# A macaron block on one core: results split by expert order, more transfer slots late in attention, row scatters issued together

## The chip, the cores and the metric

The kernel runs on one core of a Trainium2 chip. The core has a matrix engine (TensorE, here PE), a vector engine (VectorE, DVE), an activation engine (ScalarE, ACT), a general engine (GpSimd, POOL) and a queue engine (SyncE, SP), each with its own instruction stream, and 16 DMA engines that move data between the on-chip memory and HBM. Engines wait for each other through semaphores. The metric is the device time of one launch in microseconds, the median of several executions.

## The reference

The input x is eight sequences of 512 tokens with 128 features. Three steps are added to it, one after the other:

```python
x = x + 0.5 * ffn(layernorm(x), router_w, router_b, W1, b1, W2, b2)
x = x + attention(layernorm(x), w_qkv, w_o, log_xi)
x = x + 0.5 * ffn(layernorm(x), router_w, router_b, W1, b1, W2, b2)
```

`ffn` is a mixture of eight experts, each `relu(x @ W1 + b1) @ W2 + b2` with 512 hidden features. A token goes to the two experts with the highest logits, and their results are added with the softmax of the two logits as gates. `attention` is causal with 16 heads of 8 features, half of them with rotary positions, half of them with a linear decay by distance.

## The kernel before

**Rows by expert.** Each ffn runs over groups of two or three sequences: f0, f1, f2 ahead of attention and g0 (sequences 0, 1), g1 (2, 3, 4), g2 (5, 6, 7) after it. For each sequence `route` (from L801) makes the layernorm, the logits, the two chosen experts and, per token and choice, a row `g.to` in a table `xs` in HBM. Row numbers hold the expert in their lowest three bits: row = place x 8 + expert. Eight scatters a sequence (L875, an indirect DMA from POOL, 128 rows each) bring the normalised rows there. `experts` (from L924) then fetches each expert's rows (`fetch`, L933), transposes them, multiplies by W1 and W2 in "pieces" (PE lines 976, 989, 1013), and adds the bias on the way out of PSUM (L1017, on DVE, into `ysb`).

**Two ways back.** The results of f0 to f2 and g0 are written in expert order and gathered per token by indirect DMAs (`combine`). The groups g1 and g2 are "tagged": each row of `xs` carries two more values, a row number of its token (`xn[:, :, D]`, the row of the first choice) and a place for the result (`xn[:, :, D + 1]`, from `place`). `homes` (L943 to L951) finds from them, on DVE, where in `ys` the result of each row belongs: token after token, and for each token first choice, then second. `send` (L957) scatters 120 result rows at a time there, from POOL. `collect` (from L1099) reads the two results of each token back with plain DMAs from SP (L1110) and adds them to x with the gates (L1114, one instruction a choice and 128 tokens), then stores x (L1120). For g1 it does so within the run of units, for g2 at the very end, in two parts a sequence:

```python
while m.results:
    m.transfer()
last = [m.collect(g2, i, out, parts=2) for i in range(3)]
step(*last)
run(*last)
```

**Order by hand.** PE, ACT, DVE and SP execute in program order. The program is a run of units: -30 to -1 ahead of attention, 0 to 95 attention (a sequence has 12), up to 125 after it; `core` is 96, `tail` 108 and `ends` 126. `surround(n, att)` makes one unit: attention's matmuls, then a quota of pieces of the ffn group whose turn it is, mixed with what is due (routing, projections, collecting). g1 fills units 79 to 106 and g2 units 107 to 125.

**Transfers.** Indirect DMAs are not issued where they arise. Row scatters and gathers enter the queue `jobs`, result scatters the queue `results`, and `transfer()` issues one: from `jobs` first, or, with `second=True`, from `results` unless a job is urgent or there are more than four jobs and no result. A unit has two such slots, one after its first piece and one at its end; from unit `core` on a third lies in the middle if over two transfers are waiting. Each indirect DMA also waits for `mark`, the last evacuation of PSUM (or mask operation) ahead of it in the program. On POOL, scatters keep their place relative to all other instructions but not to each other. POOL also computes `rstd` of each layernorm.

**The last sequence.** Sequence 7 leaves attention in unit 98. Its routing follows in units 99 to 102, three steps a unit: statistics, `rstd`, normalisation; transposes, logits, ranks; places and gates; its eight scatters enter the queue in unit 101. g2's first rows are fetched at the end of unit 105, and the fetch waits for all scatters.

Of the kernel before, what the change touches and what calls it, by code (L numbers as in the profile page):

```python
# [11 lines left out]
FP = mybir.dt.float32  # L12
BF = mybir.dt.bfloat16
I32 = mybir.dt.int32
# [434 lines left out]
class Group:  # L449


    def __init__(self, seqs, cap, key, xs, ys, tagged):
        self.seqs, self.cap, self.key, self.xs, self.ys = seqs, cap, key, xs, ys
        self.tagged, self.width = tagged, D + 2 * tagged
        self.ct = -(-cap // P)
        self.rows = cap // self.ct
        assert self.ct * self.rows == cap
        self.parts = [(t, min(3 if cap > 4 * P else 4, self.ct - t))
                      for t in range(0, self.ct, 3 if cap > 4 * P else 4)]
        self.placed = 0  # L460
        self.pieces = E * (len(self.parts) * (1 + C) + self.ct) + 1


# [19 lines left out]
class Main:  # L483
    def __init__(self, tc, ctx, aps):
# [52 lines left out]
        for e in range(4):  # L537
# [4 lines left out]
            if e == 2:  # L542
# [48 lines left out]
                       allow_small_or_imprecise_dtypes=True)  # L591

        self.place = const.tile([P, T], FP, name="place")
        nc.gpsimd.iota(self.place, [[2 * P, T]], base=0, channel_multiplier=2,
                       allow_small_or_imprecise_dtypes=True)

        self.row = {}
# [203 lines left out]
    def route(self, g, i, urgent=False, ahead=False, early=False):  # L801
# [60 lines left out]
        for r in range(2):  # L862
            nc.vector.scalar_tensor_tensor(
                sm[:, :, r, :], rank, float(r), posb, ALU.is_equal, ALU.mult
            )
        nc.vector.tensor_reduce(g.to[:, i], sm, AX.X, ALU.max)
        nc.vector.tensor_scalar(g.back[:, i], g.to[:, i], E * g.cap - 1, None, ALU.min)
        if g.tagged:
            nc.vector.tensor_copy(xn[:, :, D], g.to[:, i, :, 0])
            nc.vector.tensor_scalar(  # L870
                xn[:, :, D + 1], self.place, float(2 * N * i), None, ALU.add
            )

        def scatter(t, r):
            ins = nc.gpsimd.indirect_dma_start(  # L875
# [35 lines left out]
        nc.vector.tensor_scalar(tot, e2, 1.0, 2.0, ALU.add, ALU.mult)  # L911
        nc.vector.reciprocal(g.gates[:, i, :, 0], tot)
        nc.vector.tensor_tensor(g.gates[:, i, :, 1], g.gates[:, i, :, 0], e2, ALU.mult)
        yield

    def close_group(self, g, k):
# [7 lines left out]
    def experts(self, g):  # L924
# [14 lines left out]
        def homes(e, xb):  # L939

            row = self.row[g.cap][:rows]
            second = self.small.tile([P, CT], FP, tag="second", name=f"second_{key}_{e}")
            nc.vector.scalar_tensor_tensor(  # L943
                second[:rows, : g.ct], xb[:rows, : g.ct, D], -float(e), row,
                ALU.add, ALU.not_equal,
            )
            nc.vector.tensor_tensor(
                second[:rows, : g.ct], second[:rows, : g.ct], xb[:rows, : g.ct, D + 1], ALU.add
            )
            home[e] = self.small.tile([P, CT], I32, tag="home", bufs=7, name=f"home_{key}_{e}")  # L950
            nc.vector.scalar_tensor_tensor(  # L951
                home[e][:rows, : g.ct], row, float(2 * N * len(g.seqs) + e),
                second[:rows, : g.ct], ALU.add, ALU.min,
            )

        def send(e, t, ys):
            ins = nc.gpsimd.indirect_dma_start(  # L957
                out=g.ys[:, :],
                out_offset=bass.IndirectOffsetOnAxis(ap=home[e][:rows, t : t + 1], axis=0),
                in_=ys[:rows, t, :], in_offset=None,  # L960
            ).ins
            tc.declare_no_dep(ins, group=f"ys_{key}", reason="no two rows have the same home")
            tc.add_to_no_dep_group(f"ys_{key}", ins)
            self.in_turn(ins, scatter=True)
            self.behind_mark(ins)

# [72 lines left out]
        for e in range(E):  # L1039
            if e + 1 < E:  # L1040
                h_next, turns, wides_next = up(e + 1, loaded.pop(0))
            else:
                turns = []

            rest = downs[:1] + turns + downs[1:]
            last = turns[-1] if turns else None
            for i, piece in enumerate(wides):
                piece()
                yield
                k = -(-len(rest) // (len(wides) - i)) if rest else 0  # L1050
                for other in rest[:k]:
                    other()
                    if other is last and e + 3 < E:
                        loaded.append(fetch(e + 3))
                    yield
                rest = rest[k:]
            downs = down(e, h)
            if e + 1 < E:
                h, wides = h_next, wides_next
        for piece in downs:  # L1060
            piece()
            yield
# [36 lines left out]
    def collect(self, g, i, dst, parts=1):  # L1099

        nc = self.nc
        b = g.seqs[i]
        x = self.x[b]
        if i % 2 == 0:
            self.pair = self.p2.tile([P, 2, T, 2, D], FP, tag="ee", name=f"yr_{b}")
        yr = self.pair[:, i % 2]
        src = g.ys[2 * N * i : 2 * N * (i + 1), :].rearrange("(t p r) d -> p t r d", p=P, r=2)
        n = T // parts
        for k in range(parts):
            nc.sync.dma_start(yr[:, ts(k, n)], src[:, ts(k, n)])  # L1110
        yield
        for t in range(T):
            for r in range(2):
                nc.vector.scalar_tensor_tensor(  # L1114
                    x[:, t, :], yr[:, t, r], g.gates[:, i, t, r : r + 1], x[:, t, :],
                    ALU.mult, ALU.add,
                )
            if t % n == n - 1:
                k = t // n
                nc.sync.dma_start(  # L1120
                    dst[b].rearrange("(t p) d -> p t d", p=P)[:, ts(k, n)], x[:, ts(k, n)]
                )
            if parts == 1:
                yield
# [179 lines left out]
def macaron_kernel(  # L1304
# [24 lines left out]
    def run(*streams):  # L1329
        for s in streams:  # L1330
            for _ in s:
                pass
# [23 lines left out]
    with ExitStack() as main:  # L1356
# [8 lines left out]
        g0 = m.open_group([0, 1], 351, 1, "g0")  # L1365
        g1 = m.open_group([2, 3, 4], 480, 3, "g1")
        g2 = m.open_group([5, 6, 7], 480, 4, "g2")
        order = [f0, f1, f2, g0, g1, g2]
        place = {True: {}, False: {}}
        for g in order:  # L1370
# [56 lines left out]
        def surround(n, att):  # L1427

            m.unit = n
            now = None  # L1430
            for g, fetch, start, end in plan:
                if n == fetch:
                    close(g)
                    fills[g.key] = [opened(g), g.pieces]
                if n == end:
                    run(fills[g.key][0])
                if start <= n < end:
                    now, until = fills[g.key], end
                    if g is g1 and att:
                        until = end + 7  # L1440
            quota = min(now[1], -(-now[1] // (until - n))) if now else 0
            fill = now[0] if now else iter(())
            if now:
                now[1] -= quota
            if att:
                ee = m.scores(*units[n])
            last, m.oT = m.oT, None
            if m.held is not None:
                got = m.values(*m.held)
                if got is not None:  # L1450
                    m.oT = (*m.held[:2], got)
            m.held = (*units[n], ee) if att else None
            m.evac = "dve" if att and n % seq not in (8, 9, 10) else "act"
            run(take(fill, 1 if quota else 0))
            m.evac = "act"
            if att:
                m.causal(units[n][2], ee, 0)
            m.transfer()
            if last is not None:
                m.outputs(*last)  # L1460
            if att:
                m.causal(units[n][2], ee, 1)
            if not att:
                m.additions()
            work = due.pop(n, [])
            todo = max(quota - 1, 0)
            for k, (stream, steps) in enumerate(work):
                some = todo // (len(work) - k + 1)
                run(take(stream, steps))
                run(take(fill, some))  # L1470
                todo -= some
            if n >= core and len(m.jobs) + len(m.results) > 2:
                run(take(fill, todo // 2))
                todo -= todo // 2
                m.transfer(second=True)
            run(take(fill, todo))
            m.additions()
            m.transfer(second=True)
# [54 lines left out]
        with m.banks(("m", 8)):  # L1533
            for u in range(core + 2, ends):
                surround(u, False)
            run(fills["g2"][0])
            assert not due, due
            assert not m.jobs and not m.adds
            while m.results:
                m.transfer()  # L1540
            last = [m.collect(g2, i, out, parts=2) for i in range(3)]
            step(*last)
            run(*last)

    flag = nc.values_load(
        bad[0:1, 0:1], min_val=0, max_val=1,
# [50 lines left out]
```

## Time and profile before

| | |
|---|---|
| median of three runs | 715.75 us (713.97 to 718.7) |
| profiled execution | 700.09 us, span 698.3 us |
| PE busy | 629.2 us (90%) |
| DVE busy | 410.2 us (59%) |
| ACT busy | 341.3 us (49%) |
| POOL busy | 300.3 us (43%) |
| result scatters, L957 | 64, 996 ns each on POOL |
| row scatters of g0 to g2, L875 | 64, 998 ns each on POOL |

The span runs from the first to the last instruction of one profiled execution. The page has the busy time of each engine and a picture of the span in 40 slices, each digit a busy share in tenths; PEclk is the clock that PE was granted, in tenths of full speed. Other answers of the trace are busy times in chosen stretches, instructions in order of time (start, duration, engine, line, operation, output and inputs, then in brackets the idle time of the engine before it and what ended it) and the chain of work that ended last, followed back from the end.

### The profile page before, as it was taken

The numbers are of one execution on the slowest core, as the hardware profiler recorded it, in microseconds if no ns is written. First come the engines' busy times: TensorE is split into PE (matmuls) and PEld (weight loads), VectorE is DVE, ScalarE is ACT, GpSimd is POOL, SyncE is SP. The second block draws the span as 40 slices with busy tenths as digits, with TensorE's granted clock in tenths as the row PEclk, the third lists the DMA queues.
The fourth block names the chain that finished last, engine by engine and source line by source line (L and its number), as shares of the span: only waits on it lengthen the run. The fifth ranks groups of instructions, "written<-read, shape, count | busy, mean of one in ns | idle before, by whom it ended". The sixth has DMA issues, their size and how long they took to land. (4 is left out here: it accounts for less than half of the span.)

```text
span 698.3 us, 13045 instructions
## 1 busy us (share of the span) xinstructions
PE 629.2 (90%) x4867; PEld 410.3 (59%) x4867; DVE 410.2 (59%) x1442; ACT 341.3 (49%) x548; POOL 300.3 (43%) x322
## 2 busy tenths in 40 slices
PE   3269999999999999999999999999999998969980
PEld 2148867756465656556656656656456656747760
DVE  6736448734466666675687677676666654433414
ACT  4034443455755656565665565555665552234420
POOL 3744637642223223314154423424144556575660
PEclk9999999999999999999999999999999999889995
DMA  8747843312409921111211111101402111145324
GB/s 265 197 136 209 205 115 98 85 45 77 101 22 172 264 69 38 30 29 43 71 32 49 40 38 38 30 27 39 105 27 75 35 31 42 53 121 140 104 58 143
DMA packets 78670, 61.06 MB, mean 87 GB/s; under 512 B 7392, under 2 KB 70792, under 8 KB 78600
## 3 DMA queue, kind: packets, MB, share of 16 engines
q1 hardware_dynamic: 69608, 42.51, 23.8%
q0 software_dynamic: 8704, 17.63, 8.5%
q8 instruction: 41, 0.67, 0.4%
q14 instruction: 29, 0.24, 0.1%
q10 hardware_dynamic: 288, 0.01, 0.0%
HBM read 26.34 MB, written 33.78 MB: 86 GB/s over the span
## 5 line engine op out<-in xcount | busy, mean ns | idle before, releaser
L1208 ACT ACTIVATE ee<-st 128x768 f32<-128x768 f32 (+1 forms) x192 | 159.0, 881 | 104.1 <-PE st L1201 100.6
L474 POOL DMA_INDIRECT yt_f<-ys,back_f x64 | 64.8, 1013 | 133.5 <-DVE ee L1215 55.7
L1215 DVE TENSOR_TENSOR ee<-ee,keep 128x256 f32<-128x256 f32 (+1 forms) x192 | 93.5, 507 | 25.4 <-ACT ee L1208 25.3
L1013 PEld LDWEIGHTS y_g<-w_sb,h_g 128*120 128x120 f32 (+1 forms) x704 | 87.1, 184 | 27.4 <-issue 21.7
L875 POOL DMA_INDIRECT xs<-xn_g,to_g x64 | 63.8, 998 | 90.1 <-DVE ee L1215 34.9
L1013 PEld LDWEIGHTS y_f<-w_sb,h_f 128*120 128x120 f32 (+1 forms) x704 | 85.9, 182 | 28.5 <-issue 16.2
L1201 PE MATMUL st<-qT,kT 32*128 32x512 f32 (+3 forms) x1024 | 96.1, 467 | 2.3 <-ACT h_f L996 0.8
L1013 PE MATMUL y_f<-w_sb,h_f 128*120 128x128 f32 (+1 forms) x704 | 93.9, 277 | 0.2 <-DVE h_f L998 0.2
L989 PE MATMUL z_g<-xT_g,w_sb 128*128 128x480 f32 (+1 forms) x192 | 92.6, 569 | 1.3 <-ACT xT_g L980 1.3
L1013 PE MATMUL y_g<-w_sb,h_g 128*120 128x128 f32 (+1 forms) x704 | 93.0, 277 | 0.6 <-DVE o_tok L1250 0.3
L1227 PE MATMUL o<-ee,vpad 128*32 128x512 f32 (+3 forms) x1024 | 89.4, 442 | 0.8 <-DVE ee L1215 0.8
L989 PE MATMUL z_f<-xT_f,w_sb 128*128 128x480 f32 (+1 forms) x192 | 88.8, 551 | 1.0 <-ACT xT_f L980 1.0
L996 ACT ACTIVATE h_f<-z_f,b1T 128x480 f32<-128x480 f32 (+1 forms) x86 | 53.5, 623 | 68.2 <-PE z_f L989 67.3
L957 POOL DMA_INDIRECT ys<-ysb_g,home_g x64 | 63.7, 996 | 39.3 <-ACT h_g L996 8.7
L1017 DVE TENSOR_TENSOR ysb_f<-y_f,b_sb 120x128 f32<-120x128 f32 (+1 forms) x88 | 25.0, 287 | 77.9 <-PE y_f L1013 74.2
L996 ACT ACTIVATE h_g<-z_g,b1T 128x480 f32<-128x480 f32 (+1 forms) x71 | 45.7, 646 | 47.4 <-PE z_g L989 46.7
L1201 PEld LDWEIGHTS st<-qT,kT 32*128 32x128 f32 x1024 | 43.1, 183 | 32.6 <-issue 8.1
L1017 DVE TENSOR_TENSOR ysb_g<-y_g,b_sb 120x128 f32<-120x128 f32 (+1 forms) x88 | 25.1, 287 | 58.2 <-PE y_g L1013 57.6
L1227 PEld LDWEIGHTS o<-ee,vpad 128*32 128x32 f32 x1024 | 23.5, 108 | 52.4 <-issue 7.5
L875 POOL DMA_INDIRECT xs<-xn_n,to_f x40 | 39.0, 974 | 34.9 <-ACT xi_sb L727 8.1
L989 PEld LDWEIGHTS z_g<-xT_g,w_sb 128*128 128x128 f32 x192 | 30.1, 195 | 26.6 <-issue 15.2
L989 PEld LDWEIGHTS z_f<-xT_f,w_sb 128*128 128x128 f32 x192 | 30.2, 194 | 13.8 <-issue 7.2
(186 smaller groups left out, 778.7 us busy)
## 6 DMA issues: line engine op xcount, KB each, us to landing
w_sb<-in_L_ffn_W_dram SPq DMA_DIRECT2D x16, 256.0 KB
xs<-zeros SPq DMA_DIRECT2D x8, 487.5 KB
xb_g<-xs SPq DMA_DIRECT2D x16, 243.8 KB
xb_f<-xs SPq DMA_DIRECT2D x16, 240.0 KB
ys<-ysb_f SPq DMA_DIRECT2D x16, 240.0 KB
ys<-zeros SPq DMA_DIRECT2D x2, 1536.0 KB
x<-in_L_attn_x_dram SPq DMA_DIRECT2D x8, 256.0 KB
xs<-zeros SPq DMA_DIRECT2D x1, 1920.0 KB
```

What stands on the lines that cost most here:

```text
L474: ins = op(*args, **kw)
L875: ins = nc.gpsimd.indirect_dma_start(out=g.xs[:, :], out_offset=bass.IndirectOffsetOnAxis(ap=g.to[:, i, t, r : r + 1], axis=0), in_=xn[:, ...
L957: ins = nc.gpsimd.indirect_dma_start(out=g.ys[:, :], out_offset=bass.IndirectOffsetOnAxis(ap=home[e][:rows, t : t + 1], axis=0), in_=ys[:r ...
L989: nc.tensor.matmul(z[:, :n], self.w1_sb[:, e, ts(c, P)], xT[:, n0 : n0 + n], start=True, stop=True,)
L996: ins = nc.scalar.activation(dst, z[:, :n], AF.Relu, bias=bias)
L1013: nc.tensor.matmul(y[:rows], h[:, c, ts(t, rows)], self.w2_sb[:, e, c, :], start=(c == 0), stop=(c == C - 1),)
L1017: ins = nc.vector.tensor_tensor(ys[:rows, t, :], y[:rows], self.b2_sb[:rows, e], ALU.add)
L1201: nc.tensor.matmul(st[:, h, c0 : c0 + N - kt * P], kT[r0 : r0 + SLOT, ts(kt, P)], qT[r0 : r0 + SLOT, kt * P :], start=True, stop=True,)
L1208: nc.scalar.activation(ee[:, two, :width], st[:, two, :width], AF.Exp)
L1215: ins = self.nc.vector.tensor_tensor(d, d, self.keep.unsqueeze(1).unsqueeze(1).to_broadcast([P, 2, len(parts), P]), ALU.min,)
L1227: self.nc.tensor.matmul(self.o[h * SLOT : (h + 1) * SLOT, kt * P :], self.vpads[b % 2][:, kt, 4 * g + h, :], ee[:, h, c0 : c0 + n], start= ...
```

## The change

It has three parts.

Results in two halves: the tag of a row becomes the row number of the token's lower-numbered expert, and the place is the token's number alone. `homes` adds the number of tokens of the group for a row of the higher expert, so that all lower results of a group lie in one half of `ys` and all higher ones in the other. The gates are swapped to match. `collect` reads the halves with one DMA each. For g2 (`g.ends`) it has more steps: the read of the lower half is issued before the last expert's W2 products, after the result queue has been emptied; expert 7 is no token's lower one, and its scatters are declared free of dependence on those reads. The higher half is read after the last scatter, then follow the additions of the lower half and those of the higher with the stores.

A third slot: the middle slot exists from unit 79 on, not from `core`.

Rows together: from unit `core + 2` on, the middle slot issues two more transfers if more than one job is waiting.

```diff
-        nc.gpsimd.iota(self.place, [[2 * P, T]], base=0, channel_multiplier=2,
+        nc.gpsimd.iota(self.place, [[P, T]], base=0, channel_multiplier=1,
...
         nc.vector.tensor_reduce(g.to[:, i], sm, AX.X, ALU.max)
+        if g.tagged:
+            which = small.tile([P, T, 2], I32, tag="which", name=f"which_{key}")
+            nc.vector.tensor_scalar(which, g.to[:, i], E - 1, None, ALU.bitwise_and)
+            swap = small.tile([P, T], FP, tag="swap", name=f"swap_{key}")
+            nc.vector.tensor_tensor(swap, which[:, :, 0], which[:, :, 1], ALU.is_gt)
+            apart = small.tile([P, T], FP, tag="apart", name=f"apart_{key}")
+            nc.vector.tensor_tensor(apart, g.to[:, i, :, 1], g.to[:, i, :, 0], ALU.subtract)
+            nc.vector.tensor_tensor(apart, apart, swap, ALU.mult)
+            nc.vector.tensor_tensor(xn[:, :, D], apart, g.to[:, i, :, 0], ALU.add)
+            nc.vector.tensor_scalar(xn[:, :, D + 1], self.place, float(N * i), None, ALU.add)
         nc.vector.tensor_scalar(g.back[:, i], g.to[:, i], E * g.cap - 1, None, ALU.min)
-        if g.tagged:
-            nc.vector.tensor_copy(xn[:, :, D], g.to[:, i, :, 0])
-            nc.vector.tensor_scalar(
-                xn[:, :, D + 1], self.place, float(2 * N * i), None, ALU.add
-            )
...
+        if g.tagged:
+            lo, hi = g.gates[:, i, :, 0], g.gates[:, i, :, 1]
+            nc.vector.tensor_tensor(tot, hi, lo, ALU.subtract)
+            nc.vector.tensor_tensor(tot, tot, swap, ALU.mult)
+            nc.vector.tensor_tensor(lo, lo, tot, ALU.add)
+            nc.vector.tensor_tensor(hi, hi, tot, ALU.subtract)
...
-            nc.vector.tensor_tensor(
-                second[:rows, : g.ct], second[:rows, : g.ct], xb[:rows, : g.ct, D + 1], ALU.add
+            nc.vector.scalar_tensor_tensor(
+                second[:rows, : g.ct], second[:rows, : g.ct], float(N * len(g.seqs)),
+                xb[:rows, : g.ct, D + 1], ALU.mult, ALU.add,
             )
...
+            if e == E - 1 and g.ends:
+                tc.declare_no_dep(ins, group="lower", reason="the last expert is none's lower")
...
+        if g.ends:
+
+            while self.results:
+                self.transfer()
+            for collect in g.ends:
+                next(collect)
         for piece in downs:
             piece()
             yield
...
-            self.pair = self.p2.tile([P, 2, T, 2, D], FP, tag="ee", name=f"yr_{b}")
+            self.pair = self.p2.tile([P, 2, 2, T, D], FP, tag="ee", name=f"yr_{b}")
         yr = self.pair[:, i % 2]
-        src = g.ys[2 * N * i : 2 * N * (i + 1), :].rearrange("(t p r) d -> p t r d", p=P, r=2)
         n = T // parts
-        for k in range(parts):
-            nc.sync.dma_start(yr[:, ts(k, n)], src[:, ts(k, n)])
-        yield
-        for t in range(T):
-            for r in range(2):
-                nc.vector.scalar_tensor_tensor(
-                    x[:, t, :], yr[:, t, r], g.gates[:, i, t, r : r + 1], x[:, t, :],
-                    ALU.mult, ALU.add,
-                )
+        src = g.ys[: 2 * N * len(g.seqs), :].rearrange(
+            "(r b t p) d -> r b p t d", r=2, b=len(g.seqs), p=P
+        )
+
+        def add(t, r):
+            nc.vector.scalar_tensor_tensor(
+                x[:, t, :], yr[:, r, t], g.gates[:, i, t, r : r + 1], x[:, t, :],
+                ALU.mult, ALU.add,
+            )
+
+        ins = nc.sync.dma_start(yr[:, 0], src[0, i])
+        if g.ends:
+            self.tc.add_to_no_dep_group("lower", ins.ins)
+            yield
+        nc.sync.dma_start(yr[:, 1], src[1, i])
+        yield
+        if g.ends:
+            for t in range(T):
+                add(t, 0)
+            yield
+        for t in range(T):
+            if not g.ends:
+                add(t, 0)
+            add(t, 1)
...
+        g2.ends = [m.collect(g2, i, out, parts=2) for i in range(3)]
...
-            if n >= core and len(m.jobs) + len(m.results) > 2:
+            if n >= 79 and len(m.jobs) + len(m.results) > 2:
                 run(take(fill, todo // 2))
                 todo -= todo // 2
                 m.transfer(second=True)
+                if n >= core + 2 and len(m.jobs) > 1:
+                    m.transfer(second=True)
+                    m.transfer(second=True)
...
-            last = [m.collect(g2, i, out, parts=2) for i in range(3)]
-            step(*last)
-            run(*last)
+            step(*g2.ends)
+            step(*g2.ends)
+            run(*g2.ends)
```

More of the change, by code (lines that the diff above doesn't have):

```diff
@@ L459, in __init__ @@
                       for t in range(0, self.ct, 3 if cap > 4 * P else 4)]
-        self.placed = 0
+        self.placed, self.ends = 0, ()
         self.pieces = E * (len(self.parts) * (1 + C) + self.ct) + 1
```

## The prediction

> **What bounds the kernel now.** I read the page's shares and slices first, then busy time by stretch near the end, then the instructions around the two holes found there, and last the chain of waits. TensorE (PE) is the bound almost everywhere; what is left lies after 580 us.
>
> ```profile
> span 698.3 us, 13045 instructions
> ...
> PE 629.2 (90%) x4867; PEld 410.3 (59%) x4867; DVE 410.2 (59%) x1442; ACT 341.3 (49%) x548; POOL 300.3 (43%) x322
> ...
> PE   3269999999999999999999999999999998969980
> ...
> PEclk9999999999999999999999999999999999889995
> ```
>
> PE stands at 9 from slice 4 to 33 (17.5 us each), so work that only moves there is worth nothing. Busy time by stretch (busy us and instruction count of PE, PEld, DVE, ACT, POOL, then granted clock, DMA share, GB/s):
>
> ```profile
> 580.00:591.00 11.00, 8.96 (x55) 6.54 (x53) 4.08 (x19) 3.12 (x5) 7.16 (x8) 1.00 0.12 37
> 591.00:598.00 7.00, 6.29 (x28) 5.29 (x29) 3.62 (x12) 1.22 (x2) 3.75 (x4) 0.52 0.13 35
> ...
> 612.00:616.70 4.70, 0.03 (x2) 0.04 (x1) 0.42 (x2) 0.00 (x0) 3.56 (x4) 0.83 0.58 145
> 616.70:622.00 5.30, 4.65 (x12) 2.78 (x13) 3.85 (x11) 1.78 (x3) 4.08 (x5) 0.50 0.82 200
> 622.00:677.50 55.50, 55.48 (x343) 41.90 (x342) 18.78 (x76) 23.86 (x37) 35.88 (x37) 1.00 0.36 97
> 677.50:698.30 20.80, 0.00 (x0) 0.00 (x0) 7.76 (x25) 0.00 (x0) 3.13 (x4) 0.56 0.42 129
> ```
>
> Three places lose time: the last sequence's routing (a stall near 589, then half clock), the wait for its rows (612 to 616.7, then half clock), and 20.8 us after PE's last matmul. GpSimd (POOL) around the second, in order of time:
>
> ```profile
> 600.92 0.99 POOL L875 DMA_INDIRECT xs<-xn_g,to_g  x1 [1.50 <-DVE ex_g L907]
> 602.22 0.98 POOL L875 DMA_INDIRECT xs<-xn_g,to_g  x1 [0.30 <-issue]
> 604.60 0.97 POOL L875 DMA_INDIRECT xs<-xn_g,to_g  x1 [1.40 <-issue]
> ...
> 610.96 0.96 POOL L875 DMA_INDIRECT xs<-xn_g,to_g  x1 [0.30 <-DMA xs<-xn_g,to_g]
> ```
>
> Eight row scatters at 1.27 us each, with one gap of 1.40 where 0.30 is normal. The last lands before SP's fetch at 613.32; PE, out of work at 612.0, restarts at 616.69. The end, from the chain of waits (start, us):
>
> ```profile
> 680.57 2.78 DMA ys<-ysb_g,home_g
> 683.37 2.52 DMA yr<-ys
> 685.91 0.36 DVE x L1114
> ```
>
> and the additions in the timeline, merged:
>
> ```profile
> 685.91 7.89 DVE L1114 SCALAR_TENSOR_TENSOR x<-yr,gates_g,x 128x128 f32<-128x128 f32 x24 [8.10 <-DMA yr<-ys]
> ```
>
> The last result scatter starts at 680.57 and has landed at 683.35; six reads follow, then 24 additions on VectorE (DVE) back to back, 7.89/24 = 0.329 us each, ending at 693.8. DVE had sat idle for 8.10 us before them.
>
> **What the Trainium skill says.** "TensorE: Matmul & The Clock Gate", part on what is actually happening: PE falls to half clock after an idle window and returns after a busy one, in windows that do not align with the kernel. The trace agrees: clock 0.52 and 0.50 in the stretches after both holes. "DMA: Bandwidth & Descriptors", anatomy of one DMA: about 2 us are fixed, mostly the confirmation of the write; here 2.78 us for the last scatter, longer. The same page, queues, rings and completion order: a DMA engine takes turns between queues packet by packet, so a scatter need not wait for all of a large read; no run here shows it. "VectorE: DVE Perf Modes", the TRN2 errata: a fixed cost per instruction outweighs the elements of small ones; this trace's operations on 4 to 8 elements per partition take 0.16 to 0.22 us, so it agrees.
>
> **The change, part by part.**
>
> *Results in a lower and a higher half.* All rows that are the lower expert's of their token come from experts 0 to 6, so their read waits only for expert 6's last scatter. By the kernel's order of slots that is the one starting at 675.40 (then four of expert 7, the last at 680.57); as with the last one, 2.78 us: landed at 678.2. A read of 256 KB in 512-byte rows is not in this trace. Bounds for the first to arrive: the old read's 2.52 us (1024-byte pieces) and 3.25 us of the expert fetch with 520-byte rows (613.32 to the first use at 616.57); the next fetch is 1.33 later. I take 3.25 and 1.33. Lower reads arrive at 681.4, 682.8 and 684.1; four additions after each are 4 x 0.329 = 1.3, so DVE is done at 685.4, in its old idle time. The queue is already empty where the change drains it (steady two to three slots for 1.75 results a unit), so draining costs nothing; and SP has only the upper reads behind the lower ones.
>
> The upper reads wait for expert 7 as before. Without disturbance: 683.37 + 3.25 = 686.6, then 12 x 0.329 = 3.9 (the arrivals, 1.33 apart, just keep pace): 690.5 to 690.6 instead of 693.8, 3.2 less. The lower reads, in flight from 678.2 to 684, now share engines with the last three scatters; I charge 0.6 (between 0, taking turns perfectly, and 3.5, should the last scatter start moving only when the lower reads have ended: 684.1 + 2.78 - 683.35). The tail: **-2.6**, between -3.9 (the whole of 12 additions) and +0.3. What covers the lower additions is DVE's 8.10 us idle time; with that cover gone they would cost 3.9 again.
>
> *Extra DVE work.* A tagged route gains four small operations before its rows may leave and four for the gates; six routes x 8 x about 0.18 = 8.6 us of DVE, five routes beside attention, where PE has 39.7 and DVE 24.7 us of work in the 40 from 520. A single PE wait for DVE there (0.80 us at 570.25) shows little room; I charge **+0.2**, bounds 0 and 1.5. In the last route three are dependent (0.20 from start to start), one is not (0.08), and one old operation moves behind: +0.6 before the scatters. An upper row's home takes one fused operation for one plain: zero.
>
> *Third slot from unit 79.* By a count of slots from the code, the queue of results at unit 98 falls from 8 to 4 and at unit 104 from 9 to 1; the last gather of sequence 1 leaves the last route's path, and with it two additions (598.05 to 598.69), -0.65. They go beside attention. This cancels the +0.6. I also looked at POOL ahead of the `rstd` power at 588.16, for which PE stalls 1.87 us: before, two scatters and a gather stand there; after, three scatters with the same marks (an evacuation each must wait for). Same rate, 1.29 a piece: the first hole stays. Other queues: collecting g1 now issues six reads for three, on SP, but may start before 633.06, and DVE's wait of 5.58 us for them (PE did not stall) should go. Zero.
>
> *Last rows in one row.* The eight scatters go four and four over units 101 and 102, not two, three, three. POOL's own rate of 1.27 stays. If the 1.40 gap came from a slot's mark, 1.1 is saved; its releaser is not named ("issue"), so between 0 and 1.1 I take **-0.7**. PE then waits some 4.0 instead of 4.67 us; its half clock stays.
>
> Sum: -2.6 + 0.2 - 0.7 = **-3.1 us**. The profiled execution took 700.09 us (span 698.3 and 1.8 around it): 697.0. The median of the runs is 715.75, 15.7 above it, which no view explains; I carry the difference over: **712.7**.
>
> **Rivals.** *Both holes shrink* (faster): POOL's order is only partly fixed, and if `rstd` runs 2.1 us earlier (its input is ready at 586.06), the 1.87 us stall goes, and half clock from 591.2 to 598 with it, worth up to 6.8/2 = 3.4. With about 3.0 of that: -3.1 - 1.9 - 3.0 = -8.0, 707.7. For it: the stall's named releaser is POOL. Against: the same number of slots ahead. *Nothing left*: smaller pieces and late scatters eat the half of the additions, and the 1.40 gap is no slot's: -2.6 and -0.7 become 0, 716.0. For it: row size; against: 8.10 us of empty DVE. *Slower*: the lower reads hold back expert 7's scatters. From a 3.2 us later landing on, the tail loses. The longest landing of a result scatter in this trace is 7.5 us, of a row scatter 10.1 (typical 2.4); at 10.1, 690.7 + 3.25 + 3.9 = 697.8, +4.0, less 0.5 from the middle: 719.3. For it: 768 KB are ahead in the same engines; against: packet-wise turns, and only four scatters. That the change doesn't do what it says is in here: were expert 7's four scatters still made to wait for the lower reads, the last would land at 684.1 + 3 x 1.29 + 2.78 = 690.8, the same.
>
> **How the numbers follow.** Forecast 0.60 (own range 710.5 to 714.5), faster rival 0.13, nothing 0.15, slower 0.12. One per cent, about what a measurement of this kernel can tell from no change, is 7.2 us: faster takes 0.10 from the first rival and 0.03 from the forecast's edge; slower takes 0.04 from the last rival with more delay and 0.05 from another half-clock stretch (3.4) on top; the rest is within. The range cuts half of each outer rival: 708 to 719.
>
> **What would show it.** Right: 12 additions before and 12 after the upper reads, ending about 3 us sooner after the last scatter; eight row scatters at 1.27 without a gap; results scattered at once near 612, DVE's 5.58 us wait gone; PE's stall near 589 as before. Wrong: the last scatter landing far over 2.8 us after its start, additions waiting between reads, PE waiting for DVE in attention, or a clock below 0.9 in a stretch that had 1.00.

## The result, and the profile after

The changed kernel took 720.12 us (median; 717.25 to 722.17), the kernel before beside it 715.83 us: a ratio of 1.0051, 95% interval 1.0032 to 1.0069. It is 0.5% slower, 4.3 us, where 3.1 us less were forecast. One thing has to be known to read the numbers below: the runs came to several devices of the same kind. On three of them the kernel before takes 701 to 702 us, on three others 716. The profile of before that the prediction was built on (700.09 us) is of the first sort; the timed comparison, and this profile of the changed kernel (720.53 us, span 718.8), are of the second. I call them the 701 and the 716 devices. By the record the experiments met devices 0, 1 and 11 of the first sort and 5, 7 and 13 of the second. Only number 11 was met twice, as a 701 device both times, so that the device and not the hour makes the difference is likely and not shown.

The page of the changed kernel:

```profile
span 718.8 us, 13100 instructions
...
PE 638.6 (89%) x4867; PEld 413.9 (58%) x4867; DVE 416.4 (58%) x1490; ACT 339.9 (47%) x548; POOL 300.8 (42%) x322
...
PE   3269989999999999999999999999998996959990
...
PEclk9999999999999999999999999999999998969995
```

PE has the same 4,867 matmul records and 9.4 us more busy time; the digits of its slices dip in more places than before. Busy time by stretch, the cuts at the same matmuls as in the prediction's table (the two stretches around the fetch of the last rows are cut at PE's stop and restart):

```profile
597.90:611.10 13.20, 10.47 (x55) 8.35 (x53) 4.76 (x19) 3.23 (x5) 6.89 (x7) 0.85 0.08 24
611.10:616.40 5.30, 5.29 (x28) 4.17 (x29) 3.17 (x12) 1.22 (x2) 2.04 (x3) 0.68 0.08 23
...
634.10:644.10 10.00, 5.17 (x12) 2.78 (x13) 4.80 (x16) 1.78 (x3) 5.65 (x7) 0.50 0.48 112
644.10:700.00 55.90, 55.90 (x342) 42.17 (x341) 18.96 (x75) 23.86 (x37) 28.88 (x30) 0.98 0.34 90
700.00:718.80 18.80, 0.29 (x3) 0.09 (x1) 7.06 (x26) 0.00 (x0) 3.56 (x4) 0.61 0.49 142
```

The last stretch is shorter, 18.8 us including 0.3 of matmuls, for 20.8. Those that rest on the last rows are longer: the 12 matmuls after the restart stand in 10.0 us where they stood in 5.3. GpSimd's row scatters of the last sequence, in order of time, no longer have the gap of 1.40 us:

```profile
619.12 1.00 POOL L880 DMA_INDIRECT xs<-xn_g,to_g  x1 [1.17 <-DVE ex_g L912]
620.42 0.98 POOL L880 DMA_INDIRECT xs<-xn_g,to_g  x1 [0.30 <-issue]
621.71 0.97 POOL L880 DMA_INDIRECT xs<-xn_g,to_g  x1 [0.30 <-issue]
...
628.09 0.97 POOL L880 DMA_INDIRECT xs<-xn_g,to_g  x1 [0.30 <-issue]
```

The chain of waits names only the last addition (713.22, `DVE x L1133`), so I read the end from VectorE's timeline:

```profile
706.24 3.24 DVE L1133 SCALAR_TENSOR_TENSOR x<-yr,gates_g,x 128x128 f32<-128x128 f32 x12 [3.98 <-DMA yr<-ys]
710.24 3.24 DVE L1133 SCALAR_TENSOR_TENSOR x<-yr,gates_g,x 128x128 f32<-128x128 f32 x12 [0.77 <-DMA yr<-ys]
```

Twelve additions stand in the time in which DVE was idle before, twelve follow the reads of the higher half, without waits between them. That is the order in the tail that was forecast. So the loss lies before PE's last matmul.

### The profile page after: what moved, and what is told of

It is laid out like the page before. It is cut to its first block, busy times and chain, and to the rows that moved or that the text cites. A ratio compares the mean times of both kernels' runs of the same rounds, so it can differ in the third digit from the quotient of the medians.

```text
span 718.8 us, 13100 instructions
## 1 busy us (share of the span) xinstructions
PE 638.6 (89%) x4867; PEld 413.9 (58%) x4867; DVE 416.4 (58%) x1490; ACT 339.9 (47%) x548; POOL 300.8 (42%) x322
## 5 line engine op out<-in xcount | busy, mean ns | idle before, releaser
L1003 PE MATMUL z_g<-xT_g,w_sb 128*128 128x480 f32 (+1 forms) x192 | 94.6, 580 | 10.4 <-ACT xT_g L994 4.8
L1003 PE MATMUL z_f<-xT_f,w_sb 128*128 128x480 f32 (+1 forms) x192 | 91.9, 568 | 1.0 <-ACT xT_f L994 1.0
L1031 DVE TENSOR_TENSOR ysb_f<-y_f,b_sb 120x128 f32<-120x128 f32 (+1 forms) x88 | 25.1, 287 | 79.3 <-PE y_f L1027 64.5
L1031 DVE TENSOR_TENSOR ysb_g<-y_g,b_sb 120x128 f32<-120x128 f32 (+1 forms) x88 | 25.1, 287 | 79.3 <-PE y_g L1027 45.5
L1010 ACT ACTIVATE h_g<-z_g,b1T 128x480 f32<-128x480 f32 (+1 forms) x71 | 45.7, 647 | 51.3 <-PE z_g L1003 41.8
```

Of the source, the lines that this page charges most:

```text
L1003: nc.tensor.matmul(z[:, :n], self.w1_sb[:, e, ts(c, P)], xT[:, n0 : n0 + n], start=True, stop=True,)
L1010: ins = nc.scalar.activation(dst, z[:, :n], AF.Relu, bias=bias)
L1031: ins = nc.vector.tensor_tensor(ys[:rows, t, :], y[:rows], self.b2_sb[:rows, e], ALU.add)
```

## The experiments

*Theory 1*: one of the change's parts costs what the prediction booked as nothing; the third slot is the suspect, since it acts from unit 79 on, in attention. *Theory 2*: the tagging on VectorE costs it. *Theory 3*, after the first runs: the parts are worth what was forecast, and the loss belongs to the device.

**Each part alone, on a 701 device.** The slot alone and the rows alone are these lines in the kernel before; the halves alone are the changed kernel with the old conditions.

```
slot alone:
-            if n >= core and len(m.jobs) + len(m.results) > 2:
+            if n >= 79 and len(m.jobs) + len(m.results) > 2:
rows alone, behind that slot's transfer:
+                if n >= core + 2 and len(m.jobs) > 1:
+                    m.transfer(second=True)
+                    m.transfer(second=True)
```

The kernel before, unchanged:

> The kernel before, unchanged, for a second profiled execution: its first one (700.09 us) lies 12.8 us under the fastest of sixteen timed runs (712.86), that of the changed kernel (720.53) in the middle of its own. Theory A (the first execution was a lucky one): span of 711 to 718 us, with stalls like those at 537, 592 and 634 us of the changed kernel, where PE's semaphore updates come 3 to 5 us after its last matmul. Theory B (those stalls are the change's): span near 700 us again and none of them. Ratio 1.000 within 0.3%.

The three parts:

> The kernel before with the third slot from unit 79 on alone. Theory 1 (the slot costs: gathers and their additions fall beside attention, DVE and SP get crowded there): 1.004 to 1.009, the whole loss. Theory 2 (the tagging costs, by DVE work in six routes and finer reads): 0.998 to 1.001. My forecast had it at zero, 1.000.

> The kernel before with the two more transfers in the middle slot from unit 98 on alone. Forecast: 0.7 us less (0.999), the 1.40 us gap between the second and third of the last eight row scatters gone. If the gap was no slot's: 1.000. If the rows held up early hold back result scatters that something waits for: over 1.001.

> The changed kernel with the slots of the kernel before: results in halves and the early read alone. Forecast: 2.4 us less (0.9966), from 2.6 at the end less 0.2 for DVE. Theory 2 (the tagging costs): 1.002 to 1.007, with the end still 2 to 2.5 us shorter after PE's last matmul and the loss before unit 96. Theory 1 (the slot costs): 0.996 to 0.998.

Measured against 701.12 us: unchanged 1.0004 (0.9993 to 1.0015), slot 0.9990 (0.9979 to 1.0001), rows 1.0001 (0.9985 to 1.0018), halves 0.9971 (0.996 to 0.9982). No part loses. The halves gain 2.0 us, the slot perhaps 0.7, the rows nothing. The gap of 1.40 us is still there with the rows alone (1.26) and gone with the slot alone: PE's wait for the last rows is 3.4 us there, and 4.2 to 5.4 in the three without the slot. What I had given to the rows is the slot's. The unchanged kernel took 701.58 here (its profile 702.12, without the stalls), so the 700.09 of the profile was no lucky execution: theory A of that run falls.

**The whole change, and the change without the halves, on a 716 device.**

> The changed kernel unchanged, beside the kernel before on the chip of this job. If the three parts add up as they did alone (0.9971 x 0.9990 x 1.0001): 0.996, the tail about 2.5 us shorter and no late semaphore updates of PE. If the parts disturb each other (a scatter that all three move, say): 1.003 to 1.007, as in the result. If a device where the kernel before takes 716 us makes the difference, the ratio follows that time: 0.996 where the kernel before takes 701, 1.005 where it takes 716.

> The kernel before with both slot changes (third slot from unit 79, two more transfers from 98), without the halves. If parts add up: 0.999, and the last eight row scatters without a gap. If slots and rows together crowd POOL before sequence 7's layernorm: 1.002 or more.

Measured against 715.74 us: the whole change 1.0063 (1.0035 to 1.009), slot and rows without the halves 1.0063 (1.0038 to 1.0087). So slot and rows together, worth 0 to -0.1% each on the other device, lose 4.5 us on this one, and VectorE's tagging (theory 2) isn't needed for it. The slot alone was never timed on a 716 device.

**The same kernels again, side by side, on another 701 device.**

> The kernel before, unchanged, for its profile where it takes about 716 us instead of 701. Theory A (the 15 us are late hand-offs: results of TensorE that VectorE and ScalarE begin on only microseconds after the last matmul ended, while GpSimd issues indirect transfers): this execution shows late hand-offs of over 0.5 us that add up to about 10 to 20 us where it takes 716, fewer than the 21 to 26 us of the changed kernel; none where it takes 701. Theory B (the device is slower throughout, for instance in its DMA or its granted clock): no such hand-offs, and the difference spread over the whole span.

> The halves of the last unit alone. It acts after TensorE's end only, so Theory A and Theory B alike expect the same 2 us as before, a ratio of 0.997 (0.9955 to 0.9985), on any device. If the ratio is 1.003 or more where the kernel before takes 716, the halves have a cost of their own there and the slot is not the cause.

> The third slot from unit 79 alone. Theory A (the slot packs GpSimd's indirect transfers closer together, and where hand-offs come late there are then more of them): 1.006 to 1.010 where the kernel before takes 716, with late hand-offs 5 to 8 us more in sum than the kernel before shows; 0.999 where it takes 701. Theory B (the rows in one row cost it): 1.000 on any device.

> The whole change. Theory A (the loss is the device's): 1.005 (1.003 to 1.008) where the kernel before takes 716, and 0.996 (0.994 to 0.998) where it takes 701, the sum of the slot's 0.999 and the halves' 0.997. Theory B (the parts hinder each other): 1.003 or more on any device.

Measured against 701.55 us: before 1.0008 (0.9998 to 1.0019), halves 0.9971 (0.996 to 0.9981), slot 0.9981 (0.9971 to 0.999), whole change **0.9954** (0.9941 to 0.9967), 3.4 us less than before. This is close to the forecast's 3.1, and to the sum of slot and halves (1.3 and 2.0): on this device the parts do not hinder each other. Whether the change gains or loses follows the sort of device.

**Late hand-offs.** In the profiles of the 716 devices, VectorE and ScalarE often begin on a result of PE long after the last matmul for it has ended. I count such hand-offs for the banks y and z of the experts: the start of the evacuation, less the later of the last matmul's end and the end of the previous instruction on the same engine, where that is over 0.5 us. Of 368 evacuations, no profile on a 701 device has a single one. The changed kernel's has 15 on its 716 device, 26.1 us in sum; the two runs above have 11 (21.5) and 13 (24.0). All lie at 85 to 155 us and from 554 us on, each with two or more indirect transfers of GpSimd between 4 us before it was due and its start. Not every close row brings one: in the changed kernel six from 125.71 to 133.1 us, 0.30 us apart, pass without, though evacuations of y and z fall among them. The count leaves out the banks of attention and of the transposed rows (`xbT_ps`). (Matmul ends are modelled, as "Perfetto Trace Analysis" of the Trainium skill says in its part on Tensor Engine instructions, which also puts the update of the semaphore after PSUM's acknowledgement. No view here separates a late acknowledgement from a late update.)

Two more runs for the kernel before's own profile on a 716 device came to a 701 device:

> The kernel before, unchanged, again for its profile where it takes about 716 us. Theory A (late hand-offs from TensorE on that device cost the 15 us): late hand-offs of over 0.5 us that add up to 10 to 20 us, fewer than the 21.5 to 26.1 us of the changed kernel there. Theory B (a device slower throughout): none. Where it takes 701, both expect none.

> The halves alone. Theory A (the slot brings the loss): 0.997 (0.9955 to 0.9985) where the kernel before takes 716 as well as where it takes 701. Theory B (the gain at the end is lost on that device): 1.000 or more where the kernel before takes 716.

They gave 701.3 us without a late hand-off, and 0.9964 (0.9953 to 0.9976).

**Dense transfers where there were none.** This adds indirect gathers to the kernel before in the middle of attention:

```
+    def spares(self, n):
+        for k in range(2):
+            self.nc.gpsimd.indirect_dma_start(
+                out=self.spare[:, (2 * n + k) % 4], out_offset=None,
+                in_=self.aps["x"].rearrange("b n d -> (b n) d"),
+                in_offset=bass.IndirectOffsetOnAxis(ap=self.plain[:, 0:1], axis=0),
+            )
...
             m.transfer()
+            if 20 <= n < 60:
+                m.spares(n)
```

> The kernel before with two more indirect gathers behind each other in every unit from 20 to 59 (rows of the input x into a tile that nothing reads), so that GpSimd is as densely busy there, at about 210 to 430 us, as it is at 90 to 150 and 540 to 640. Theory A (late hand-offs come with dense indirect transfers on a device where the kernel before takes 716): there late hand-offs appear between 210 and 430 us, where the changed kernel had none, 5 to 15 us in sum, and the ratio is 1.007 to 1.02. Theory B (they belong to the stages, not to the transfers): none there, ratio 1.000 to 1.003. Where the kernel before takes 701, both expect no late hand-off and 1.000 to 1.004, the upper end if GpSimd's own work is held up by the added transfers.

> The halves alone; up to TensorE's end its trace is that of the kernel before. Theory A (the slot brings the loss where the kernel before takes 716, and late hand-offs are why): there 0.997 (0.9945 to 0.9995), with 10 to 20 us of late hand-offs, fewer than the 21.5 to 26.1 us of the kernels with the slot. Theory B (the gain at the end is lost there): 1.000 or more, and as many late hand-offs as with the slot. Where the kernel before takes 701, both expect 0.997 and none.

A miss, on a 701 device: 788.77 us, 1.1246 (1.1226 to 1.1266). The added gathers wait for nothing and stand in no order, and the profile has all of them between 8 and 176 us, ahead of their units; PE waits once for 27.0 and once for 54.1 us there, both times for normalised rows from VectorE (`xnT_ps_f`). The halves beside it: 0.9981 (0.997 to 0.9993), no late hand-off. The next run puts each added gather into the order of the others:

```
+            self.in_turn(ins, scatter=True)
+            self.behind_mark(ins)
```

> As the run before with the two added gathers of each unit from 20 to 59 bound into the order of the other transfers, so that they run in their units (about 210 to 430 us) and no longer ahead of the row scatters of earlier stages. Up to 210 us and from 540 us on it is the kernel before. Theory A (dense indirect transfers bring the late hand-offs where the kernel before takes 716): there 5 to 15 us of them between 210 and 430 us and a ratio of 1.007 to 1.02. Theory B (they belong to the stages): none there and 1.000 to 1.003. Where the kernel before takes 701, no late hand-off and 1.000 to 1.004 under both.

> The halves alone, again for a device where the kernel before takes 716: 0.997 (0.9945 to 0.9995) with fewer late hand-offs than the slot's 21.5 to 26.1 us under Theory A (the slot brings the loss); 1.000 or more and as many under Theory B (the gain at the end is lost there). Where it takes 701: 0.997 and none.

This came to a 716 device (715.87 us). With the added gathers 764.88 us, 1.0688 (1.0657 to 1.0719). Busy time of about the same span of units, in the halves and then in this kernel, whose program is the kernel before's there but for the gathers:

```profile
210.00:432.00 222.00, 219.62 (x1886) 131.03 (x1884) 150.51 (x485) 128.69 (x207) 69.56 (x68) 1.00 0.27 70
```

```profile
210.00:480.00 270.00, 235.72 (x1873) 136.32 (x1876) 150.16 (x472) 128.17 (x206) 149.26 (x148) 0.94 0.29 77
```

POOL's busy time rises from 70 to 149 us, the stretch is 48 us longer, and PE's longest waits there are for evacuations:

```profile
PE z_f L1003 <- DVE ysb_f L1031: 8.4, 3, 4.4
PE y_g L1027 <- DVE h_g L1012: 7.8, 3, 3.9
PE xbT_ps_g L990 <- DVE h_g L1012: 4.8, 2, 4.1
```

Late hand-offs now stand between 257 and 466 us, up to 4.9 us each, where the kernels without added gathers have none (the nearest is one of 0.64 us in the halves, at 485). That they come with dense transfers is what theory A said; the gathers' price, 49 us, is three to ten times what it said, and how much of it the late hand-offs make wasn't separated from POOL's own time. The halves: 1.0025 (1.0002 to 1.0048), where theory A had 0.997, and 34.6 us of late hand-offs in 21, more than any kernel with the slot. These are the numbers of that run's theory B. So theory A's measure falls: the slot doesn't raise the sum of late hand-offs, and the halves seem to have a loss of their own on this device. What the slot does must be sought place by place.

**The kernel before on a 716 device.**

> The kernel before with two more indirect gathers in every unit from 20 to 59, bound into the order of the transfers, a second time; it took 764.9 us where the kernel before takes 716, with 48 us lost between 210 and 480 us at hand-offs that came up to 4.9 us late. Theory A (the late hand-offs are a property of some devices and are brought about there by dense indirect transfers): where the kernel before takes 701, no late hand-off and 702 to 706 us, a ratio of 1.001 to 1.007. Theory B (the added transfers cost 48 us by themselves, by occupying GpSimd): 740 us or more on any device. Where the kernel before takes 716, both expect 765 again.

> The kernel before, for its profile where it takes 716 us. Theory A (the third slot adds one late hand-off near 540 us, which the three profiles with the slot have and the one with the halves alone has not): late hand-offs near 90 to 150 and 590 to 670 us, none between 530 and 560. Theory B (it is chance): one near 540 too. Where it takes 701, none at all.

Again a 716 device (716.38). The kernel with added gathers took 759.94 us, 1.0596 (1.0539 to 1.0653), so it has no run on a 701 device in its bound form; how much of its 44 to 49 us the gathers would cost there is open. The kernel before, profiled at 718.22 us, has 12 late hand-offs, 20.9 us in sum, near 80 to 150 and from 587 us on, none between. Its profile can be laid beside the changed kernel's matmul by matmul (us; the stretches are cut at the same matmuls, counted in the order of time; each column is one execution, the two of the 716 sort of different jobs):

| Stretch | before, 701 | after, 701 | before, 716 | after, 716 |
|---|---|---|---|---|
| first 3,722 matmuls | 507.1 | 505.9 | 513.5 | 514.1 |
| next 217 | 24.9 | 24.9 | 24.9 | 25.1 |
| next 125 | 15.4 | 15.4 | 15.5 | **20.5** |
| next 275, to the last route | 34.7 | 34.7 | 37.1 | 38.2 |
| next 186, last route and fetch of its rows | 42.4 | 41.8 | 48.6 | 46.2 |
| last 342 | 55.1 | 55.5 | 55.8 | 56.2 |
| after PE's last matmul | 20.9 | 18.1 | 21.0 | 18.5 |
| span | 700.5 | 696.3 | 716.4 | 718.8 |

On the 701 device the change takes 2.8 us from the tail and leaves the rest within 1.2 a stretch. On the 716 device it takes 2.5 from the tail, gives 5.0 in one stretch of 15 us, and all else sums to nearly nothing. That stretch is 20.6 us in the run with slot and rows too, and 15.5 with the halves alone. Its lines from the windows, before and after on a 716 device, then after on a 701 device, and last the part of the second behind the stall:

```profile
538.40:553.90 15.50, 15.50 (x127) 8.42 (x125) 9.52 (x35) 9.65 (x14) 7.07 (x7) 1.00 0.31 76
```

```profile
539.20:559.70 20.50, 17.21 (x127) 8.77 (x124) 9.76 (x36) 10.95 (x16) 10.23 (x11) 0.92 0.32 80
```

```profile
530.80:546.20 15.40, 15.40 (x127) 8.44 (x125) 9.41 (x37) 9.64 (x14) 10.49 (x11) 1.00 0.42 104
```

```profile
543.50:547.00 3.50, 3.46 (x25) 1.12 (x26) 1.27 (x9) 2.03 (x3) 2.75 (x3) 0.54 0.33 98
```

The same matmuls, with PE 3.3 us idle and partly at half clock. GpSimd just ahead of it, in the timeline of the kernel before (716):

```profile
532.51 0.99 POOL L875 DMA_INDIRECT xs<-xn_g,to_g  x1 [0.31 <-issue]
535.00 0.98 POOL L875 DMA_INDIRECT xs<-xn_g,to_g  x1 [1.50 <-DVE recs L1249]
536.62 0.97 POOL L875 DMA_INDIRECT xs<-xn_g,to_g  x1 [0.64 <-DVE x L1073]
539.96 1.17 POOL L875 DMA_INDIRECT xs<-xn_g,to_g  x1 [2.37 <-DVE ee L1215]
...
537.95 0.66 DVE L982 COPY xT_g<-xbT_ps_g 128x480 f32<-128x480 f32 x1 [0.96 <-PE xbT_ps_g L976]
```

and of the changed kernel (716), with PE, VectorE and ScalarE behind it:

```profile
532.24 0.99 POOL L880 DMA_INDIRECT xs<-xn_g,to_g  x1 [1.15 <-DVE ee L1249]
533.53 0.97 POOL L880 DMA_INDIRECT xs<-xn_g,to_g  x1 [0.30 <-DVE x L1093]
...
537.47 0.97 POOL L880 DMA_INDIRECT xs<-xn_g,to_g  x1 [0.30 <-DVE x L1093]
538.74 0.97 POOL L880 DMA_INDIRECT xs<-xn_g,to_g  x1 [0.31 <-issue]
...
537.93 0.63 PE L990 MATMUL xbT_ps_g<-ident,xb_g 120*128 120x120 f32 x4
...
541.08 0.66 DVE L996 COPY xT_g<-xbT_ps_g 128x480 f32<-128x480 f32 x1 [3.29 <-remote]
...
541.01 1.51 ACT L1242 ACTIVATE ee<-st 128x768 f32<-128x768 f32 x2 [7.05 <-PE kT_ps L1212]
...
541.79 1.07 PE L1003 MATMUL z_g<-xT_g,w_sb 128*128 128x480 f32 x2 [2.35 <-DVE xT_g L996]
```

("remote" is an end of a wait for which the view has no releaser.) Before, the slots leave 0.6 to 2.4 us between scatters here. With the third slot six follow each other at 0.30. The transpose of `xb_g` has ended at 538.56; its evacuation begins at 541.08, 2.5 us later (in the kernel before 0.2). ScalarE waits beside it, for scores that ended near 537.2. The trace has PE's semaphore updates at 536.50 and then at 540.93, 541.05, 541.11 and 541.17: four updates were due between 537.2 and 539.4, by the matmuls' ends, and they come within 0.24 us. ScalarE and VectorE start within 0.15 us of the first. PE, in program order, waits meanwhile: it stops for 2.35 and 0.68 us and goes on at half clock (0.54). On the 701 device the changed kernel issues the same six scatters as closely, and nothing happens:

```profile
523.70 0.98 POOL L880 DMA_INDIRECT xs<-xn_g,to_g  x1 [0.81 <-DVE ee L1249]
524.98 0.97 POOL L880 DMA_INDIRECT xs<-xn_g,to_g  x1 [0.30 <-DVE x L1093]
...
530.19 0.97 POOL L880 DMA_INDIRECT xs<-xn_g,to_g  x1 [0.30 <-issue]
...
530.25 0.66 DVE L996 COPY xT_g<-xbT_ps_g 128x480 f32<-128x480 f32 x1 [0.81 <-PE xbT_ps_g L990]
```

All three profiles with the slot on 716 devices have this stall (PE's wait for `xT_g` is 2.35, 2.37 and 2.35 us); none of the four without the slot (before, halves and twice the added gathers) has it. The rows can't be its cause: they act from unit 98 on, and attention, which ends ahead of that, has its last scores at 581 us in the changed kernel. The slot alone packs these scatters so on a 701 device (its lines follow), and the rows alone do not:

```profile
523.95 0.98 POOL L875 DMA_INDIRECT xs<-xn_g,to_g  x1 [0.81 <-DVE ee L1215]
525.23 0.97 POOL L875 DMA_INDIRECT xs<-xn_g,to_g  x1 [0.30 <-DVE x L1073]
...
530.45 0.96 POOL L875 DMA_INDIRECT xs<-xn_g,to_g  x1 [0.30 <-issue]
```

So the last run's theory A stands: the slot adds one late hand-off near 540 us. What in the slot does it is not shown, for it moves more than scatters. SP's fetches of rows start at 538.34 in the changed kernel, as the late hand-off falls due (538.56), and in the kernel before (716) at 542.43, well behind the same hand-off (537.95):

```profile
538.34 4.04 SPq L944 DMA_DIRECT2D xb_g<-xs  x3
```

```profile
542.43 1.16 SPq L933 DMA_DIRECT2D xb_g<-xs  x2
```

In favour of the scatters, a hand-off in the changed kernel also came 2.8 us late at 629 us, where the DMA engines were busy to 0.15 (625 to 629 us). No run separates the two.

## Why the prediction was wrong

**Half of the additions in DVE's idle time, -2.6**: right in mechanism and, in part by luck, in size. The tail lost 2.8 us on a 701 device and 2.5 on a 716 device; the halves alone gave -2.0, -2.0, -2.5 and -1.3 by their four ratios on 701 devices. The terms inside it were off and cancel. On the 701 device of the table twelve additions take 3.3 us where I had 3.9, and the upper reads take from issue to the first addition within 0.1 us of the old ones' time, where I had charged 0.7 more; but the last scatter is waited for 0.9 us longer (charged 0.6), and from the last addition to the end of the span it is 0.9 longer, which was not in the sum. If that first 0.9 is what the lower reads cost expert 7's scatters, it is far below the 3.2 from which the slower rival had the tail lose, so that rival has no part in the loss.

**Extra DVE work, +0.2**: not contradicted on 701 devices, open on 716 devices (below). The new small groups take 153 to 174 ns an instruction, about as charged. PE's stall near `rstd` is 1.9 us in both kernels on both sorts of device, as forecast.

**Rows in one row, -0.7**: the size was about right and the part wrong. The rows alone gave nothing; the gap of 1.40 goes with the slot, which alone gave -0.7 and -1.3 us by its two ratios. What in the slot closes the gap stays open.

**Third slot, zero**: this step failed. On a 701 device it was a small gain; on a 716 device the stretch with its stall costs 5.0 us (the profiles), and slot and rows together 4.5 (the medians). I had counted what GpSimd's transfers wait for, and what waits for them, and asked nothing about what a closer row of them, or reads that come forward with it, may do to hand-offs between other engines. The prediction's own list of signs had it under "wrong": "PE waiting for DVE in attention" is what the stretch shows, and its clock fell from 1.00 to 0.92, not quite to the 0.9 given there. VectorE's wait for g1's reads (5.58 us in the profile of before, 3.15 in the later one on a 701 device) is gone, as forecast, and moved nothing.

**The carrying over, 697.0 to 712.7**: this failed with it. The 15.7 us between profile and median was no constant of the measurement. On such a device the kernel before loses 15.8 us up to PE's last matmul and 0.1 in the tail (the table). Of the largest single steps two, 5.4 and 1.8 us, lie where PE stops behind a late hand-off of transposed rows to ScalarE (635.5 and 589.5 us); the third, 1.6, where it waits longer for fetched rows (94.2). Smaller ones I did not follow one by one. A profile of a 701 device can't show how a change moves them. "Which no view explains" was the warning: the sum was good where its profile came from (698.12 against 701.55, ratio 0.9954; forecast 0.9956), and was applied to a machine whose profile I had not seen.

What stays open. The stretch near 540 us and the tail leave a loss of 2.5 us, the profiles' spans one of 2.4; the medians have 4.3 and 4.5. So some 2 us of the loss are in no place that is shown here. The halves may have a part in them: in medians on a 716 device they alone lost 1.8 us (0.1 to 3.4) although their tail is 2.8 us shorter in the profile, and the whole change lost no less than slot and rows without them. The expectations of two runs say that the halves act only after TensorE's end; that is not so, as their tags and gates add DVE instructions in six routes. In the one pair of profiles PE ends 1.6 us later than in the kernel before, in no single place, and I can't say why. Why the updates come late on some devices wasn't found: whether PE, PSUM or the path of the semaphores is behind, or the recording itself. Every execution on record, timed or profiled, has a span and a granted clock and so left records, and the traces of 716 devices lack some; no run shows these devices without it. Nor is it known whether the bound gathers of the last experiment would cost anything on a 701 device. Of the versions that were timed on both sorts none beats the kernel before on both: the whole change is the fastest on 701 devices, the kernel before on 716 devices.

## What to carry to other kernels

If a profile and the timed median differ by more than their scatter, as here by 2%, find the reason before a sum from one is carried to the other; a profile of the device that is timed may show waits that the other hasn't. Closing the gaps between GpSimd's indirect transfers is not free merely because nothing waits for them: look at the hand-offs between other engines at the same time. And the gain at the end, half of the last additions in idle time, held best: it came out within 0.2 us of the forecast in the profiles of both sorts. The halves' median on a 716 device does not show it, so a gain seen in one place of a profile is not yet one of the whole.

## What the runs showed of the hardware

- On three devices the kernel before took 701 to 702 us, on three others 716; on the latter 11 to 21 evacuations (without added gathers) began 0.5 to 7.5 us late, on the former none of 368.
- There, several of PE's semaphore updates came together after a silence (536.50, then four from 540.93 to 541.17). The traces of these devices also hold fewer records: for the kernel before 4,521 of landings of transfers and 780 of PE's semaphore updates, on a 701 device 6,725 and 889.
- Two more indirect gathers a unit over 40 units cost 44 to 49 us on 716 devices, with PE's longest waits there for evacuations by VectorE.
- Eighty gathers that depend on nothing ran some 200 us and more ahead of their units and cost 87 us on a 701 device, with one wait of PE of 54.1 us.
